# A scheduler's clock count, its refinements, and two buffers, in a state-space scan followed by window attention

## The chip, the cores and the metric

The kernel runs on one core of a Trainium2 chip, in float32. The metric is the time of one execution on the device in microseconds; lower is better. Each kernel is run several times, and the median counts. One execution per kernel is also recorded by the hardware profiler. In the profile PE is TensorE's products, PEld its weight loads, DVE is VectorE, ACT ScalarE, POOL GpSimd, and SP the engine that issues the transfers.

## The reference, cut to what matters

Input x is 8 images of 192 channels, 64x64. Two layers follow each other.

```python
# layer 0
x  = conv1x1(x, W_in)                     # 192 -> 384 channels
x  = depthwise3x3(x) + b_dw
p  = conv1x1(x, W_xd)                     # 16 values per point
ws, Ls, Us, Ds = (conv1x1(p, w) for w in (W_w, W_l, W_u, W_d))
xs = stack(x, x.T, flip(x), flip(x.T))    # 4 directions x 384 channels
Gl, Gm, Gr = split(ws)
s  = abs(Gl) + abs(Gm) + abs(Gr) + 1e-7   # each gate is divided by s
for t in range(8):                        # steps within chunks of 8 columns
    h = Ls*xs + (Gl*h_up + Gm*h + Gr*h_dn) / s
    out[t] = h*Us + xs*Ds
y  = sum over directions of w_m[d] * out[d]
y  = layernorm over channels(y)
y  = grn(y)                               # needs the sum of y*y over the image
x  = conv1x1(y, W_out)                    # 384 -> 192

# layer 1
s0 = layernorm(tokens of x)
for each window of 8x8 tokens, for each of 6 heads:
    a = l2norm(q) @ l2norm(k).T * temperature
    a = where(a >= 16th largest of its row, a, -100)
    o = softmax(a + rpb) @ v
x2 = s0 + proj(o)
out = x2 + fc2(gelu(fc1(layernorm(x2))))  # 192 -> 768 -> 192
```

## The kernel before

**Three streams.** For each image there is a *front* (input projection, depthwise convolution as products on TensorE over strips read back from DRAM), a *scan*, and eight *window rows* of attention and feed-forward, each 8 image rows of 512 tokens. While image b is scanned, the front of image b+1 and the window rows of image b-1 are written beside it. The window rows of an image can begin only when its scan has ended, since the normalisation needs a sum over the whole image.

**The scan.** A tile is one direction, 128 channels and 512 points at one step t: 12 tiles a step, 8 steps an image, 768 tiles in all. For t above 0 a tile goes so. TensorE makes four products, three into PSUM banks named g and one into the bank nb (`gates`, L681); nb comes from a pool of two banks of its own (`n_ps`), all others of a pool of six. DVE multiplies by the input (L730) and by the state (L745, L747), ACT takes absolute values (L738, L760), POOL adds two of them (L769), DVE the third into nb (L777), so nb holds the normaliser. ACT makes the first reciprocal (L780, L782), POOL adds the products and multiplies (L784, L788, L799), DVE refines (L795, L803) and writes the new state (L810). After every second tile TensorE makes four output products for the pair (`both`, in `outputs`), and DVE (L836, L841) and POOL (L848 to L858) add them to the sum over directions.

**The window rows.** In order: scaling and W_out (L1040, L1055), normalisation, transposes (L1020), q and k (L1105), v (L1144), normalising q and k (L1179), their transposes (L1192, copied out by L1200), scores (L1220), top 16 on DVE (L1247 to L1264), softmax, transposes (L1321), product with v (L1341), projection (L1375), norm, transposes (L1443, L1445), widening (L1462, L1466) into `hd`, gelu (L1482), narrowing (L1496) and output.

**What sets the order.** None of this is issued in the order in which it is written. Each step is noted with its engine, its cost and the buffers that it reads and writes (`plan`, class `Plan`); a buffer is a `Held`, made by its first user and given back when its last user in the plan has run. `Plan.order` then lays out all steps with a list scheduler: on each engine it takes, of the steps that can start soonest, the one with the lowest rank. After each run a step's rank is set to the start of what needs it first, less its own length, and the plan is run again, `RUNS` times; the shortest is kept. All five engines' instructions are issued in that order. The hardware's semaphores are put in from what the instructions really touch, so a wait that only the plan has shapes the order and nothing else.

**The clock in the plan.** A PE step has a cost of a lead in ns, a number of cycles, and a share. `run` counts `cycles * share` in windows of `TICK` ns; in a window whose predecessor counted `ENTRY` or more, PE runs at 2.4 cycles per ns, else at 1.2. The costs are lambdas near L460: `mm`, `tiled`, `split`, `turned`, `mg`.

**The two buffers.** `outputs` got the second tile's `nb` and named it as read by the step `both`, though the function `both` does not touch it. The transposed q and k of a row lay in two buffers of tag `four`, 96 partitions of 2 x 512 values each; the hidden layer `hd` is one buffer of 128 x 6 x 512.

Of the kernel before, what the change touches and what calls it, by code (L numbers as in the profile page):

```python
# [54 lines left out]
class Held:  # L55
# [11 lines left out]
    def __call__(self):  # L67
        return self.tile
# [9 lines left out]
class Plan:  # L78
# [5 lines left out]


    HOP = 35.0
    TICK, ENTRY = 10240 / 3, 3060.0
    RUNS = 12
    SLACK = 40.0

    def __init__(self):
# [1 line left out]
        self.parts = {}  # L93
        self.rank, self.lane = 0.0, 0

    def __call__(self, engine, cost, fn, r=(), w=()):
        s = Step(engine, fn, cost, self.rank, self.lane, len(self.steps))
        self.steps.append(s)
        deps = set()
        for item in r:  # L100
            for k in self._overlaps(item, self.writers):
                deps.update(self.writers[k])
        for item in w:
            for k in self._overlaps(item, self.writers):
                deps.update(self.writers[k])
            for k in self._overlaps(item, self.readers):
                deps.update(self.readers[k])
        for item in list(r) + list(w):
            h = item[0] if isinstance(item, tuple) else item
            if isinstance(h, Held) and s not in h.users:  # L110
                if not h.users:
                    s.makes.append(h)
                else:
                    deps.add(h.users[0])
                h.users.append(s)
                s.held.append(h)
                h.left += 1
        for item in w:
            for k in self._overlaps(item, self.readers):
                if k == item or not isinstance(item, tuple):  # L120
                    self.readers[k] = []
            if not isinstance(item, tuple):
                for k in self._overlaps(item, self.writers):
                    self.writers[k] = []
            self.writers[item] = [s]
        for item in r:
            self.readers.setdefault(item, []).append(s)
        self._index(list(r) + list(w))
        deps.discard(s)
        s.before = len(deps)  # L130
        for d in deps:
            d.after.append(s)
        return s
# [12 lines left out]
    def order(self):  # L146

        before = [s.before for s in self.steps]
        tiles = {h: h.left for s in self.steps for h in s.held}
        best = None
        for _ in range(self.RUNS):
            for s, k in zip(self.steps, before):
                s.before, s.ready = k, 0.0
            for h, k in tiles.items():
                h.left, h.end, h.next = k, 0.0, None  # L160
            run = self.run()
            if best is None or self.length < best[0]:
                best = self.length, run, [s.start for s in run]
            for s in run:
                needs = [d.start for d in s.after] + [h.next.start for h in s.held if h.next]
                s.rank = min(needs, default=s.end) - (s.end - s.start)
        self.length, run, starts = best
        for s, t in zip(run, starts):
            s.start = t
        return run  # L170
# [118 lines left out]
def tile_ss2d_then_window_attention(ctx: ExitStack, tc: tile.TileContext, a: dict, out: bass.AP):  # L289
# [170 lines left out]
    vec = lambda n: (n / 0.96 + 69, 88)  # L460
    act = lambda n, more=50.0: (n / 1.2 + more, 110)
    gp = lambda n: (n * 2.3 + 52, 42)
    mm = lambda slots, n, share=1.0: (65.0, slots * n * 4.16, share)
    tiled = lambda cycles, share=1.0: (150.0, cycles, share)
    split = (275.0, 6475.0, 1.0)
    turned = lambda n, share=1.0: (60.0, 262.0 * n, share)

    mg = lambda share=1.0: (120.0, 2270.0, share)
    dma = lambda n=1, kb=0: (max(350.0 * n, 5.4 * kb), 2600.0)
    tiny = (150.0, 60.0)  # L470
    log_c = {}
# [144 lines left out]
    def scan(b, xs, xsT, z, made):  # L616
# [68 lines left out]
        def tile_of(t, d, ct, xp, x0, y3, last):  # L685
# [85 lines left out]
            if last:  # L771
                last()

            def rest():
                if t > 0:
                    rr = Held(spool, [P, 512], "rr", bufs=2)
                    plan("DVE", vec(512), lambda: nc.vector.tensor_add(nb(), nb(), ab()[:, 0, :]), r=[ab], w=[nb])  # L777

                    plan(
                        "ACT", (581.0, 110.0), lambda: nc.scalar.activation(rr(), nb(), AF.Ln, bias=eps7), r=[nb], w=[rr]  # L780
                    )
                    plan("ACT", act(512, 95.0), lambda: nc.scalar.activation(rr(), rr(), AF.Exp, scale=-1.0), w=[rr])  # L782
                    one = lambda: pr()[:, 0, :]
                    plan("POOL", gp(512), lambda: nc.gpsimd.tensor_add(one(), one(), pr()[:, 1, :]), r=[(pr, 1)], w=[(pr, 0)])  # L784
                    plan(
                        "POOL",
                        gp(512),
                        lambda: nc.gpsimd.tensor_add(one(), one(), pr()[:, 2, :]),  # L788
                        r=[(pr, 2)],
                        w=[(pr, 0)],  # L790
                    )
                    plan(
                        "DVE",
                        vec(512),
                        lambda: nc.vector.scalar_tensor_tensor(nb(), nb(), 1e-7, rr(), ALU.add, ALU.mult),  # L795
                        r=[rr],
                        w=[nb],
                    )
                    plan("POOL", gp(512), lambda: nc.gpsimd.tensor_mul(one(), one(), rr()), r=[rr], w=[(pr, 0)])  # L799
                    plan(  # L800
                        "DVE",
                        vec(512),
                        lambda: nc.vector.scalar_tensor_tensor(nb(), nb(), 2.0, one(), ALU.subtract, ALU.mult),  # L803
                        r=[(pr, 0)],
                        w=[nb],
                    )
                    plan(
                        "DVE",
                        vec(512),
                        lambda: nc.vector.tensor_sub(state(d, ct), like(lx(), d), like(nb(), d)),  # L810
                        r=[lx, nb],
                        w=[h_key],
                    )
                waiting.append((d, ct, xd, xv, h_key))
                if len(waiting) == 2:
                    outputs(waiting, nb if t > 0 else None)

            def outputs(pair, nb):

                banks = [[bank("g") for _ in range(2)] for _ in range(2)]  # L820

                at = PAIRS.index(tuple(p[:2] for p in pair)) * P

                def both():
                    for k in range(2):
                        for m in range(2):
                            project(banks[k][m](), w_g2, 64 * k + RG * m, RG, at, xp())

                plan("PE", mg(), both, r=[xp, nb] if nb else [xp], w=banks[0] + banks[1])
                for (d, ct, xd, xv, h_key), (pd, pu) in zip(pair, banks):  # L830
                    onto_sum(d, ct, xd, xv, h_key, pd, pu)
                pair.clear()
# [31 lines left out]
        def norm(t, y3):  # L864
# [22 lines left out]
            m4 = Held(spool, [P, P], "m4", tag="xq", bufs=1)  # L887
            plan("PE", tiled(1553.0), lambda: means(pm, y3), r=[y3], w=[pm])
            plan("ACT", act(P), lambda: nc.scalar.copy(m4(), pm()[:, 0:P]), r=[pm], w=[m4])
            plan("PE", tiled(2203.0), lambda: spread(pm, m4), r=[m4], w=[pm])  # L890
            plan(
                "DVE",
                vec(1536),
# [26 lines left out]
                r=[pv],  # L920
                w=[sq],
            )
            plan("PE", tiled(2203.0), lambda: spread(pv, rr), r=[sq], w=[pv])
            plan(
                "DVE",
                vec(1536),
# [85 lines left out]
    def window_row(b, g, z, sc, bb):  # L1012
# [170 lines left out]
        plan("DVE", (2373.0, 90.0), unit, r=[nn], w=[qk])  # L1183
        yield
        plan.lane = 8
        qkT = [Held(lpool, [HALF, 2, GT], "four", bufs=2) for _ in range(2)]
        for k in range(4):
            pt = bank()

            def turn(k=k, pt=pt):  # L1190
# [2 lines left out]
                        pt()[0:HALF, tt * P : (tt + 1) * P], qk()[:, tt, k * HALF : (k + 1) * HALF], ident  # L1193
                    )

            plan("PE", turned(4), turn, r=[qk], w=[pt, (qkT[k // 2], "room")])
            plan(
                "ACT",
                act(512),
                lambda k=k, pt=pt: nc.scalar.copy(qkT[k // 2]()[:, k % 2, :], pt()[0:HALF, :]),  # L1200
                r=[pt],
                w=[(qkT[k // 2], k % 2)],
            )
            yield

# [8 lines left out]
        def scores():  # L1214
            for w in range(WS):
                tok = slice(w * 64, w * 64 + 64)
                for r in range(3):
                    rows = slice(32 * r, 32 * r + 32)
                    for j in range(2):
                        nc.tensor.matmul(  # L1220
                            pas[r]()[64 * j : 64 * j + 64, tok],
                            lhsT=qkT[0]()[rows, j, tok],
                            rhs=qkT[1]()[rows, j, tok],
                            start=True,
                            stop=True,
                        )

        plan("PE", tiled(2550.0, 0.6), scores, r=qkT, w=pas + [(at, "room")])
        for r in range(3):
            rng = slice(r * WS, (r + 1) * WS)  # L1230
            plan(
# [114 lines left out]
                                stop=True,  # L1346
                            )

        plan("PE", tiled(2350.0, 0.5), attend, r=[at, v], w=po + [("oT", "room")])
        for w in range(2):  # L1350
            plan(
                "ACT",
# [288 lines left out]
```

## Time and profile before

| | |
|---|---|
| median of 3 runs | 7846.2 us (7838.49 to 7853.48) |
| the profiled execution | 7831.69 us, its span 7829.6 us |
| mean granted TensorE clock | 0.849 |
| busy PE, PEld | 6807.6, 3516.3 us |
| busy DVE, ACT, POOL | 6279.8, 4911.0, 6212.0 us |
| instructions | 144584 |
| read and written in HBM | 453.43 and 232.67 MB |

Busy times are the union of an engine's instructions. The ends of products are modelled, so a busy PE is not PE at its peak; the granted clock says in tenths of full speed at what rate it ran. In the list of waits each line has the waiting engine, tile and line, then what ended the wait, then us in total, number of waits and the longest. Line numbers are those of the kernel before.

### The profile page before, as it was taken

Reading aid. Unit: us, or ns where it says so; the run is one execution under the profiler, and the core shown is the slowest. Engines: PE = TensorE matmul, PEld = TensorE weight load, DVE = VectorE, ACT = ScalarE, POOL = GpSimd, SP = SyncE. Lnnn points to the kernel's source line nnn. Section 1 sums busy time; section 2 is a strip of 40 time slices with the busy share of each in tenths; the row PEclk is TensorE's granted clock in tenths of the full one; section 3 lists DMA queues with packets and bytes.
Section 4 is the critical chain, followed back from the end, with each engine's and each line's share of the span. In section 5 each row is a group of like instructions: output and inputs, shape, how many; then the busy total and the mean of one; then the engine's idle time right before and its main releaser. Section 6 shows DMA issues by size and latency. Waiting matters only on the chain.

```text
span 7829.6 us, 144584 instructions
## 1 busy us (share of the span) xinstructions
PE 6807.6 (87%) x51224; PEld 3516.3 (45%) x51224; DVE 6279.8 (80%) x15421; ACT 4911.0 (63%) x9657; POOL 6212.0 (79%) x6302
## 2 busy tenths in 40 slices
PE   5788888888999889889998889988888898788888
PEld 2333344444444444444444444444444444344554
DVE  1377778899788978889889888888899989999443
ACT  1355446775666656766677656767566656666665
POOL 0388878899788978888889878888799989899332
PEclk8788779987898878888898779988878878788998
DMA  7666445312543135322553124431211121111110
GB/s 183 181 170 167 125 123 146 100 50 65 151 115 78 47 112 137 87 69 59 140 141 85 44 85 129 115 80 51 58 48 49 50 61 51 46 47 46 25 25 14
DMA packets 1037929, 695.53 MB, mean 89 GB/s; under 512 B 704116, under 2 KB 860215, under 8 KB 1037207
## 3 DMA queue, kind: packets, MB, share of 16 engines
q1 hardware_dynamic: 1035830, 684.99, 33.0%
q8 instruction: 407, 6.67, 0.4%
q14 instruction: 316, 2.58, 0.1%
q10 hardware_dynamic: 1376, 1.30, 0.1%
HBM read 453.43 MB, written 232.67 MB: 88 GB/s over the span
## 4 chain that ended last, share of the span: by engine, by line
DVE 21%; PE 19%; POOL 15%; ACT 8%; issue 4%; DMA 0%; POOLq 0%; SPq 0%; ACTq 0%; DVEq 0%
PE g L681 6%; PE lp L1496 4%; POOL pr L799 3%; POOL ab L769 2%; POOL pr L784 2%; DVE rest L1249 2%; POOL dx L850 2%; PE lp L1105 2%; POOL pr L788 2%; DVE pr L745 2%; DVE nb L803 1%; DVE pr L747 1%; PE lp L1462 1%; POOL y L858 1%; DVE top L1247 1%
## 5 line engine op out<-in xcount | busy, mean ns | idle before, releaser
L681 PE MATMUL g<-xe,w_g 32*128 32x512 f32 x3648 | 1273.0, 768 | 271.1 <-DVE dx L836 106.9
L681 PE MATMUL g<-xo,w_g 32*128 32x512 f32 x3648 | 1156.1, 728 | 218.5 <-DVE dx L836 123.8
L784 POOL TENSOR_TENSOR pr<-pr 128x512 f32<-128x512 f32 x672 | 878.0, 1307 | 192.7 <-DVE pr L745 137.1
L769 POOL TENSOR_TENSOR ab<-ab 128x512 f32<-128x512 f32 x672 | 873.3, 1300 | 162.6 <-ACT ab L738 157.8
L738 ACT ACTIVATE ab<-g 128x512 f32<-128x512 f32 x1344 | 782.2, 596 | 333.3 <-PE nb L681 145.7
L799 POOL TENSOR_TENSOR pr<-pr,rr 128x512 f32<-128x512 f32 x672 | 869.2, 1294 | 125.7 <-ACT rr L782 106.9
L788 POOL TENSOR_TENSOR pr<-pr 128x512 f32<-128x512 f32 x672 | 865.4, 1289 | 17.2
L850 POOL TENSOR_TENSOR dx<-dx,hu 128x512 f32<-128x512 f32 x576 | 738.2, 1290 | 121.8 <-DVE hu L841 108.2
L780 ACT ACTIVATE rr<-nb,eps 128x512 f32<-128x512 f32 x672 | 461.3, 686 | 566.5 <-DVE nb L777 564.4
L681 PEld LDWEIGHTS g<-xe,w_g 32*128 32x128 f32 x3648 | 447.3, 216 | 811.2 <-DVE dx L836 227.8
L568 PE MATMUL lp<-strip,w_cv 128*32 128x256 f32 x9216 | 682.0, 440 | 142.5 <-DMA strip<-pad 123.5
L681 PEld LDWEIGHTS g<-xo,w_g 32*128 32x128 f32 x3648 | 390.9, 206 | 731.5 <-DVE dx L836 250.2
L1496 PE MATMUL lp<-hd,w_f 128*64 128x256 f32 (+1 forms) x2304 | 585.1, 492 | 33.7 <-ACT hd L1482 23.6
L795 DVE SCALAR_TENSOR_TENSOR nb<-nb,rr 128x512 f32<-128x512 f32 x672 | 464.5, 691 | 186.8 <-ACT rr L782 185.9
L858 POOL TENSOR_TENSOR y<-y,dx 128x512 f32<-128x512 f32 x384 | 593.4, 1554 | 2.2
L803 DVE SCALAR_TENSOR_TENSOR nb<-nb,pr 128x512 f32<-128x512 f32 x672 | 464.4, 691 | 152.0 <-POOL pr L799 149.7
L777 DVE TENSOR_TENSOR nb<-nb,ab 128x512 f32<-128x512 f32 x672 | 464.5, 691 | 110.3 <-POOL ab L769 94.2
L568 PEld LDWEIGHTS lp<-strip,w_cv 128*32 128x32 f32 x9216 | 304.5, 123 | 543.0 <-issue 274.3
L848 POOL TENSOR_TENSOR y<-hu,dx 128x512 f32<-128x512 f32 x192 | 252.6, 1320 | 340.6 <-DVE hu L841 337.9
L841 DVE TENSOR_TENSOR hu<-g,hid 128x512 f32<-128x512 f32 x768 | 517.8, 678 | 4.9 <-PE g L681 4.4
L681 PE MATMUL nb<-xe,w_g 32*128 32x512 f32 x672 | 511.9, 852 | 11.1 <-DVE hid L810 8.8
L760 ACT ACTIVATE nb<-nb 128x512 f32<-128x512 f32 x672 | 398.7, 593 | 183.6 <-DVE pr L745 107.7
(203 smaller groups left out, 16680.0 us busy)
## 6 DMA issues: line engine op xcount, KB each, us to landing
strip<-pad SPq DMA_DIRECT2D x1152, 132.0 KB
xd<-xsT SPq DMA_DIRECT2D x384, 256.0 KB
pad<-xin SPq DMA_DIRECT2D x192, 264.0 KB
xs<-st SPq DMA_DIRECT2D x192, 256.0 KB
xsT<-sn SPq DMA_DIRECT2D x192, 256.0 KB
xd<-xs SPq DMA_DIRECT2D x192, 256.0 KB
x<-xs SPq DMA_DIRECT2D x64, 768.0 KB
z<-y SPq DMA_DIRECT2D x64, 768.0 KB
```

The costliest lines, as they stand in the source:

```text
L568: nc.tensor.matmul(pc()[q * RG : (q + 1) * RG, k * 256 : (k + 1) * 256].rearrange("p (h w) -> p h w", h=4), lhsT=w_cv[:, ct, q, dx, :], rh ...
L681: nc.tensor.matmul(dst, lhsT=w[rows, col : col + P], rhs=xp[rows, :], start=True, stop=True)
L738: lambda r=r: nc.scalar.activation(ab()[:, r, :], g[r](), AF.Abs),
L769: plan("POOL", gp(512), lambda: nc.gpsimd.tensor_add(ab()[:, 0, :], ab()[:, 0, :], ab()[:, 1, :]), w=[ab])
L784: plan("POOL", gp(512), lambda: nc.gpsimd.tensor_add(one(), one(), pr()[:, 1, :]), r=[(pr, 1)], w=[(pr, 0)])
L788: lambda: nc.gpsimd.tensor_add(one(), one(), pr()[:, 2, :]),
L799: plan("POOL", gp(512), lambda: nc.gpsimd.tensor_mul(one(), one(), rr()), r=[rr], w=[(pr, 0)])
L803: lambda: nc.vector.scalar_tensor_tensor(nb(), nb(), 2.0, one(), ALU.subtract, ALU.mult),
L841: lambda: nc.vector.tensor_mul(like(hu(), d), like(pu(), d), state(d, ct)),
L850: plan("POOL", gp(512), lambda: nc.gpsimd.tensor_add(dx(), dx(), hu()), r=[hu], w=[dx])
L858: nc.gpsimd.tensor_add(y, y, dx().rearrange("p (c i) -> p i c", c=CH))
L1496: nc.tensor.matmul(dst[:, at : at + rhs.shape[-1]], lhsT=lhsT, rhs=rhs, **flags)
```

## The change

The planner's shares: full products from 1.0 to 0.96, 0.95 or 0.9, two kinds of `tiled` to 0.93, the product with v from 0.5 to 0.65. `ENTRY` goes from 3060 to 3200. `RUNS` goes from 12 to 30, and from the second run on a rank is the mean of the old and the new. `plan` takes steps in `behind`, after which a step must come without a buffer between them: `both` is now put behind the step that made the last value of nb (L803), and no longer holds nb. The four transposed blocks of q and k become one buffer of 96 x 4 x 512 under the tag `hd`, the same single buffer that the hidden layer uses.

```diff
-    TICK, ENTRY = 10240 / 3, 3060.0
-    RUNS = 12
+    TICK, ENTRY = 10240 / 3, 3200.0
+    RUNS = 30
...
-    def __call__(self, engine, cost, fn, r=(), w=()):
+    def __call__(self, engine, cost, fn, r=(), w=(), behind=()):
...
-        deps = set()
+        deps = set(behind)
...
-        for _ in range(self.RUNS):
+        for n in range(self.RUNS):
...
-                s.rank = min(needs, default=s.end) - (s.end - s.start)
+                rank = min(needs, default=s.end) - (s.end - s.start)
+                s.rank = (s.rank + rank) / 2 if n else rank
...
-    mm = lambda slots, n, share=1.0: (65.0, slots * n * 4.16, share)
+    mm = lambda slots, n, share=0.96: (65.0, slots * n * 4.16, share)
...
-    split = (275.0, 6475.0, 1.0)
+    split = (275.0, 6475.0, 0.95)
...
-    mg = lambda share=1.0: (120.0, 2270.0, share)
+    mg = lambda share=0.9: (120.0, 2270.0, share)
...
+            made_w = []
...
-                    plan(
-                        "DVE",
-                        vec(512),
-                        lambda: nc.vector.scalar_tensor_tensor(nb(), nb(), 2.0, one(), ALU.subtract, ALU.mult),
-                        r=[(pr, 0)],
-                        w=[nb],
+                    made_w.append(
+                        plan(
+                            "DVE",
+                            vec(512),
+                            lambda: nc.vector.scalar_tensor_tensor(nb(), nb(), 2.0, one(), ALU.subtract, ALU.mult),
+                            r=[(pr, 0)],
+                            w=[nb],
+                        )
                     )
...
-                    outputs(waiting, nb if t > 0 else None)
+                    outputs(waiting, made_w)
...
-                plan("PE", mg(), both, r=[xp, nb] if nb else [xp], w=banks[0] + banks[1])
+                plan("PE", mg(), both, r=[xp], w=banks[0] + banks[1], behind=made_w)
...
-            plan("PE", tiled(2203.0), lambda: spread(pm, m4), r=[m4], w=[pm])
+            plan("PE", tiled(2203.0, 0.93), lambda: spread(pm, m4), r=[m4], w=[pm])
...
-            plan("PE", tiled(2203.0), lambda: spread(pv, rr), r=[sq], w=[pv])
+            plan("PE", tiled(2203.0, 0.93), lambda: spread(pv, rr), r=[sq], w=[pv])
...
-        qkT = [Held(lpool, [HALF, 2, GT], "four", bufs=2) for _ in range(2)]
+        qkT = Held(lpool, [HALF, 4, GT], "four", bufs=1, tag="hd")
...
-            plan("PE", turned(4), turn, r=[qk], w=[pt, (qkT[k // 2], "room")])
+            plan("PE", turned(4), turn, r=[qk], w=[pt, (qkT, "room")])
...
-        plan("PE", tiled(2550.0, 0.6), scores, r=qkT, w=pas + [(at, "room")])
+        plan("PE", tiled(2550.0, 0.6), scores, r=[qkT], w=pas + [(at, "room")])
...
-        plan("PE", tiled(2350.0, 0.5), attend, r=[at, v], w=po + [("oT", "room")])
+        plan("PE", tiled(2350.0, 0.65), attend, r=[at, v], w=po + [("oT", "room")])
```

## The prediction

> **What bounds the kernel now.** I read the page from the top, then the busy time by stretches, then the waits of VectorE and TensorE.
>
> ```profile
> span 7829.6 us, 144584 instructions
> ## 1 busy us (share of the span) xinstructions
> PE 6807.6 (87%) x51224; PEld 3516.3 (45%) x51224; DVE 6279.8 (80%) x15421; ACT 4911.0 (63%) x9657; POOL 6212.0 (79%) x6302
> ...
> PEclk8788779987898878888898779988878878788998
> ...
> DVE 21%; PE 19%; POOL 15%; ACT 8%; issue 4%; DMA 0%; POOLq 0%; SPq 0%; ACTq 0%; DVEq 0%
> ```
>
> No engine is full. PE leads at 87%, DVE and POOL follow at 80 and 79%, and the chain that ended last runs over all three, none with more than 21%. DMA holds none of it. The TensorE clock is below full in every slice. So time is lost where engines take turns, which is what an order of instructions decides.
>
> ```profile
> core 0: us, PE busy (x) PEld busy (x) DVE busy (x) ACT busy (x) POOL busy (x), PEclk, DMA share, GB/s
> 330.00:1200.00 870.00, 735.61 (x4910) 319.90 (x4910) 667.98 (x1065) 460.32 (x824) 726.38 (x592) 0.77 0.56 148
> ...
> 3000.00:3900.00 900.00, 821.28 (x6255) 424.06 (x6255) 778.09 (x1906) 601.13 (x1177) 774.14 (x775) 0.87 0.35 93
> ...
> 5700.00:6600.00 900.00, 791.10 (x5352) 417.71 (x5349) 822.68 (x2067) 598.83 (x1204) 816.53 (x834) 0.83 0.18 51
> ...
> 7253.00:7830.00 577.00, 483.40 (x4461) 306.79 (x4460) 262.88 (x1282) 364.87 (x779) 169.64 (x363) 0.91 0.10 22
> ```
>
> Four stages with different limits: the first image's scan without attention beside it (clock 0.77); the steady part (PE 91%, DVE and POOL 86%); from 5700 us, when the front has no image left, DVE and POOL at 91% and PE at 88%; and after the last scan update at 7253 us a tail of 577 us in which PE is busy 84% and the others much less.
>
> ```profile
> ACT rr L780 <- DVE nb L777: 564.4, 356, 8.1
> ...
> PE g L681 <- DVE dx L836: 230.7, 142, 6.7
> ...
> DVE nb L795 <- ACT rr L782: 185.9, 159, 4.4
> ...
> DVE nb L803 <- POOL pr L799: 149.7, 162, 4.2
> ...
> ACT four L1200 <- PE lp L1192: 55.6, 51, 3.5
> ...
> PE nb L681 <- DVE hid L810: 19.4, 14, 3.1
> ```
>
> The numbers after the colon are us in total, times, and the longest. ScalarE's 564 us are its own slack (63% busy). What costs are DVE's waits inside a tile (L795, L803), and PE waiting until DVE has read a bank (L836). PE's wait for the normaliser's bank, the one that the change speaks of, is 19.4 us in all.
>
> **The change part by part.** I compared the two instruction orders engine by engine. The same instructions are there on every engine (26,894 TensorE products before splitting, 13,887 on DVE, 9,221 on ACT, 6,305 on POOL, 2,966 on SP): nothing is added or taken away, no DMA either. Everything is order, so each part is costed by what it does to the order.
>
> *The normaliser's bank.* The product step of a pair never touches the bank in its code; naming it only kept the planner from reusing the bank early. The chip has no such wait to lose. At most PE's 19.4 us for that bank (and 51.5 us of weight loads) could change; at least nothing. The order says nothing: at 376 of 384 pairs exactly one further tile's gates stand ahead of the pair's products, before and after, and the gates follow the products at once 312 times before and 311 after. Value 0.
>
> *One buffer for the transposed q, k and the hidden layer.* It adds a wait: the copies into it (L1200) and behind them the scores, the top-k on DVE and the mask may not start while the hidden layer of the row before is in use. In the old order 9 of 63 rows overlapped so. In the new one 62 rows have their scores ahead of the first widening product and one follows the last narrowing product, so the wait lies satisfied in PE's own order. A row held back by the life of the hidden layer (4.4 tiles on average; 768 tiles in 6,908 us are 9.0 us each, so 40 us) costs only if the last rows are later. Eleven rows' wide layers are left when the scan's last product is issued, in both orders. Value 0; bounds 0 and one row more in the tail, 577/11 = 52 us.
>
> *The clock's counting.* It takes no cycle from PE; it only tells the planner which windows run at full rate. From the trace I summed, over the 3.413 us windows between the recorded clock changes, the cycles of each step by the planner's own table. Threshold 3060 with the old shares foresees the next window's rate in 94.5% and calls 71.5% full; 69.6% were. Threshold 3200 with the new shares: 93.9%, and 65.1% full. So the new planner takes PE for somewhat slower than it is, an error that gives PE's steps room and costs no more than that room. Here the page "TensorE: Matmul & The Clock Gate" of the Trainium skill speaks against the change (Part 1, on the HAM clock gate): the window runs freely and isn't reset when a kernel starts, and the warm-up costs under 1% of a typical kernel's span. By the first, no plan can aim at windows counted from its own time zero, and I follow it: value 0 by intent. By the second no clock effect could pass 78 us. Here the trace differs: mean clock 0.849, so some 30% of the time is at half rate. If half of the time is bound by PE (58 of 110 six-tile stretches below), 0.01 of clock is worth 0.01/0.849 of 6,908 x 58/110, or 43 us. I keep that for the range.
>
> *30 refinements, ranks averaged.* Here the order itself is the only evidence. I gave each instruction its mean duration from the trace's groups (PE's scaled to its 6,807.6 us busy) and measured three things in both orders.
>
> Balance: cut the scan into stretches of N tiles, take for each the engine with the most work, and add up. N=2: 7134 before, 7120 after; N=4: 6767 and 6769; N=6: 6534 and 6509; N=12: 6325 and 6309. The differences are -14, +2, -25, -16 us. Four tiles' inputs can be waiting beside a pair that waits for its outputs, so I lean to six: -20 us.
>
> Cover on DVE: between L777 and L795 of a tile the work of ACT (0.69 + 0.63 us and two handovers of 0.15, as the timeline has them, 1.62 us together) must be hidden by other DVE work. The shortfall summed over 672 tiles is 123 us in the old order (the trace shows 185.9) and 134 in the new. From L777 to L803 (POOL's 1.29 us more) it is 61 and 71. That is 10 us more; DVE is the fullest engine in a quarter of the stretches, and partly elsewhere, so I take +4 us. On POOL (L769 to L799) 23 and 25: nothing. For PE's banks, the time until a bank comes round again falls short by 429 and 424 us: nothing.
>
> Tail: of PE's work 455.7 us stood behind the last scan product and now 444.3, so 11.4 us go into the body. At 84% busy that shortens the tail by 13 us and lengthens the body, bound by PE about half of the time, by 6: -7 us. The head is the same: the same products stand ahead of the first scan product.
>
> Sum: -20 + 4 - 7 + 0 = -23 us. The profiled execution took 7831.7 us (span 7829.6 and 2.1 around it) and would become 7808.7. The median of the runs before is 14.5 us above that execution, so against it: 7846.2 - 23 = **7823 us**, 0.3% less.
>
> **The rivals.**
>
> *The clock comes out higher.* If the reordering closes gaps between products, more windows count as busy. For it: every slice of the page has half-rate windows, and the first scan runs at 0.77. Against it: the density of products is nearly the same (gaps of no other step between two scan steps: 473 before, 461 after). At 0.01 more clock it gives 7823 - 43 = 7780 us; at 0.02, 7737.
>
> *Slower: thinner cover in DVE's queue.* A plan is shorter because dependent steps stand closer. Between L777 and L803 of a tile there are 6.44 us of other DVE work before and 6.30 after, 0.14 us less in each of 672 tiles, 94 us in sum. The plan thinks that this is free; on the chip products and activations come at times shifted by a clock window, and a wait then opens at L795 or L803. With half of it paid, the term of +4 becomes +47, the sum +20, and the time 7866 us; with all of it 7913. It decides from the point where those two waits grow by more than the 27 us that balance and tail bring. For it: these two waits are already 336 us. Against it: ACT is idle 37% of the time, and most tiles have cover to spare.
>
> *The change doesn't do what it says.* The early bank and the shared buffer leave no mark in the order; then they count nothing and the time is the forecast's, from ranks alone. I hold this to be so.
>
> **How the numbers follow.** Forecast (small gain from ranks and tail) 0.52, own range 7795 to 7850; higher clock 0.26; thinner cover 0.22. A measurement of this kernel tells about 0.2%, 16 us, from no change. Faster by more than that (under 7830.5): 0.36 of the forecast's chance and all 0.26 of the clock's, 0.62. Slower by more (over 7861.9): 0.20 of the cover's and 0.02 of the forecast's, 0.22. Between: 0.16. The range goes down through the clock case to a little past its 0.01 (7765) and up past the half-paid cover (7880), short of a whole row more in the tail; about 0.1 lies beyond each end.
>
> **What would show it.** Right: busy times and counts of every group as before within a few us; the last scan update (L810) near 7240 us instead of 7253.5; the tail about 565 us; waits at L795 and L803 together within 20 us of 336; clock 0.845 to 0.855. Wrong for the forecast: clock of 0.86 or more with a PE busy time well under 6,800 us (the clock case), or those two waits above 380 us with DVE's busy time unchanged (the cover case). L1200 or L1473 waiting for the shared buffer, or a tail of over 600 us, would say that the buffer costs after all. PE's wait for L810 staying near 19 us would confirm that freeing the bank early does nothing.

## The result and the profile after

The changed kernel takes 7777.7 us (median of 4 runs, 7769.28 to 7784.22) against 7842.3 for the kernel before in the same runs: ratio 0.9918, 95% interval 0.9899 to 0.9937. So it is 0.8% faster, about 64 us. The forecast was 0.3% faster and a range from 7765 to 7880: the side and the range hold, the size is well under half. The profiled execution took 7776.0 us.

The page of the changed kernel, span, busy times, clock and chain:

```profile
span 7774.2 us, 144512 instructions
## 1 busy us (share of the span) xinstructions
PE 6784.8 (87%) x51224; PEld 3499.8 (45%) x51224; DVE 6280.8 (81%) x15421; ACT 4902.0 (63%) x9657; POOL 6208.0 (80%) x6302
...
PEclk8888778888898889888898889988788878888998
...
DVE 29%; PE 29%; POOL 20%; ACT 9%; issue 6%; DMA 1%; SPq 0%; POOLq 0%; DVEq 0%; ACTq 0%
```

The chain of before adds up to 67% of the span and this one to 94%, so their shares can't be compared. The counts of instructions on the five compute rows are the same, and the busy times of DVE, ACT and POOL agree within 9 us. Nothing became cheaper; the same work lies closer together. PE has 23 us less busy time at a mean clock of 0.853 (0.849 before).

Where the time went is seen by cutting both executions at the first and the last state update of the scan. These are the stretches between them, before and then after (columns: stretch, length, busy us of PE, PEld, DVE, ACT, POOL, clock, DMA share, GB/s):

```profile
345.50:7253.50 6908.00, 6102.43 (x44990) 3108.46 (x44990) 5963.56 (x14032) 4471.86 (x8772) 6007.50 (x5908) 0.85 0.34 90
```

```profile
337.80:7217.40 6879.60, 6097.55 (x45042) 3104.68 (x45045) 5965.19 (x14038) 4466.64 (x8782) 6003.27 (x5910) 0.85 0.34 90
```

The first update starts 7.7 us earlier, the stretch is 28.4 us shorter with DVE and POOL as busy as before within 5 us (DVE's idle time falls from 944 to 914 us), and what follows the start of the last update shrinks from 576 to 557 us. By stage after the change:

```profile
core 0: us, PE busy (x) PEld busy (x) DVE busy (x) ACT busy (x) POOL busy (x), PEclk, DMA share, GB/s
330.00:1200.00 870.00, 715.96 (x4958) 308.32 (x4947) 676.48 (x1101) 464.45 (x833) 734.58 (x604) 0.79 0.57 150
...
3000.00:3900.00 900.00, 823.49 (x6404) 422.44 (x6406) 786.74 (x1926) 604.40 (x1205) 781.67 (x789) 0.87 0.37 98
...
5700.00:6600.00 900.00, 788.83 (x5594) 426.05 (x5589) 818.12 (x2072) 596.06 (x1218) 812.67 (x834) 0.84 0.19 52
...
7218.00:7774.00 556.00, 473.50 (x4406) 297.83 (x4402) 261.41 (x1275) 360.72 (x767) 168.78 (x361) 0.92 0.10 22
```

In the first scan DVE and POOL get some 8 us more work done in the same 870 us, at a clock of 0.79 instead of 0.77, and in the steady part 9 and 8 us more in the same 900 us; in the stage without a front they get no more. The tail has 10 us less of PE's work. The waits after (lines moved by 1 to 5):

```profile
ACT rr L783 <- DVE nb L780: 577.2, 367, 7.5
...
PE g L682 <- DVE dx L841: 201.1, 116, 7.7
...
DVE nb L798 <- ACT rr L785: 187.1, 161, 3.9
...
DVE nb L807 <- POOL pr L802: 162.6, 174, 4.1
...
ACT four L1205 <- PE lp L1197: 67.5, 59, 3.7
...
PE nb L682 <- DVE hid L815: 16.6, 12, 3.3
```

The two waits inside a tile come to 350 us (336 before), PE's wait for a bank that DVE has to read to 201 (231), and the wait for the normaliser's bank to 16.6 (19.4). One of DVE's waits in the window rows is shorter too, that for the squares of q and k, before and then after:

```profile
DVE nn L1128 <- ACT sq L1121: 187.8, 71, 19.6
```

```profile
DVE nn L1133 <- ACT sq L1126: 164.7, 88, 14.1
```

So two waits fell by 23 and 30 us, others rose, and none accounts for the 64 us.

### The profile page after: what moved, and what is told of

Same layout as the page of the kernel before. It is cut to its first block, busy times and chain, and to the rows that moved or that the text cites. A ratio compares the mean times of both kernels' runs of the same rounds, so it can differ in the third digit from the quotient of the medians.

```text
span 7774.2 us, 144512 instructions
## 1 busy us (share of the span) xinstructions
PE 6784.8 (87%) x51224; PEld 3499.8 (45%) x51224; DVE 6280.8 (81%) x15421; ACT 4902.0 (63%) x9657; POOL 6208.0 (80%) x6302
## 4 chain that ended last, share of the span: by engine, by line
DVE 29%; PE 29%; POOL 20%; ACT 9%; issue 6%; DMA 1%; SPq 0%; POOLq 0%; DVEq 0%; ACTq 0%
PE g L682 9%; PE lp L1501 5%; POOL pr L802 4%; POOL ab L770 3%; POOL pr L787 3%; POOL pr L791 3%; POOL dx L855 3%; DVE pr L746 3%; DVE rest L1254 2%; PE lp L1110 2%; DVE nb L807 2%; PE lp L569 2%; DVE pr L748 2%; DVE hid L815 2%; DVE nb L780 2%
## 5 line engine op out<-in xcount | busy, mean ns | idle before, releaser
L682 PE MATMUL g<-xe,w_g 32*128 32x512 f32 x3648 | 1234.9, 756 | 267.7 <-DVE dx L841 98.0
L682 PEld LDWEIGHTS g<-xe,w_g 32*128 32x128 f32 x3648 | 424.8, 212 | 799.2 <-DVE dx L841 198.1
L569 PE MATMUL lp<-strip,w_cv 128*32 128x256 f32 x9216 | 666.0, 430 | 124.6 <-DMA strip<-pad 114.6
```

The lines of the kernel that those rows point to most:

```text
L569: nc.tensor.matmul(pc()[q * RG : (q + 1) * RG, k * 256 : (k + 1) * 256].rearrange("p (h w) -> p h w", h=4), lhsT=w_cv[:, ct, q, dx, :], rh ...
L682: nc.tensor.matmul(dst, lhsT=w[rows, col : col + P], rhs=xp[rows, :], start=True, stop=True)
```

## The experiments

Ratios are to the kernel before, measured on the same chip beside each kernel. The first four take one part of the change alone.

**The clock's count alone.**

```diff
-    TICK, ENTRY = 10240 / 3, 3060.0
+    TICK, ENTRY = 10240 / 3, 3200.0
-    mm = lambda slots, n, share=1.0: (65.0, slots * n * 4.16, share)
+    mm = lambda slots, n, share=0.96: (65.0, slots * n * 4.16, share)
...
```

> The kernel before with the new threshold (3200) and shares alone; 12 refinements, ranks not averaged, both buffers as before. Ranks theory (the prediction's: the gain is from the refinements, the clock's count is worth nothing): within 15 us of before, 7827 to 7857. Clock theory (the stricter count lays a better order): most of the 65 us, 7770 to 7795. Shuffle theory (every new order is a draw, parts do not add): anything from 7800 to 7880. Followed through the plan's own arithmetic, this order is 51 us longer than before's under the old constants and 76 us shorter under the new ones, so the sign tells which constants describe the chip.

Measured: 7847.8 us, ratio 1.0001 (0.9992 to 1.0009). The count alone brings nothing; the clock theory falls in its plain form. The sign that was to tell which constants describe the chip didn't come, neither +51 nor -76.

**The refinements alone.**

```diff
-    RUNS = 12
+    RUNS = 30
...
+                s.rank = (s.rank + rank) / 2 if n else rank
```

> The kernel before with 30 refinements and averaged ranks alone. Ranks theory: all of the gain, 7775 to 7800. Clock theory: within 15 us of before. Shuffle theory: 7800 to 7880. The plan's arithmetic says 27 us shorter than before under the old constants, 62 us shorter under the new.

Measured: 7817.7 us, ratio 0.9966 (0.9954 to 0.9978): 27 us, less than half of the gain. Both the theory that gives all of it to the ranks and the plain clock theory fall; the range of the shuffle theory holds.

**The normaliser's bank alone.**

```diff
-                plan("PE", mg(), both, r=[xp, nb] if nb else [xp], w=banks[0] + banks[1])
+                plan("PE", mg(), both, r=[xp], w=banks[0] + banks[1], behind=made_w)
```

> The kernel before with only the normaliser's bank given back by the output products (they stand behind the last write to it instead). Ranks and clock theory: no wait of the chip is touched, so within 15 us of before. Shuffle theory: it moves all the same, since the order is laid anew, by more than 15 us either way. The plan's arithmetic: 3 us longer under the old constants, 38 us shorter under the new.

Measured: 7834.5 us, ratio 0.9989 (0.9979 to 0.9999). About 9 us, at the edge of what can be told from nothing. The shuffle theory asked for more than 15 us either way, and misses.

**The shared buffer alone.**

```diff
-        qkT = [Held(lpool, [HALF, 2, GT], "four", bufs=2) for _ in range(2)]
+        qkT = Held(lpool, [HALF, 4, GT], "four", bufs=1, tag="hd")
```

> The kernel before with only the transposed q and k moved into the hidden layer's buffer. Ranks and clock theory: value 0, within 15 us of before; if the shared buffer costs, slower by up to 52 us. Shuffle theory: moves by more than 15 us either way. The plan's arithmetic: 14 us shorter under the old constants, 7 us shorter under the new.

Measured: 7834.9 us, ratio 0.9988 (0.9981 to 0.9996). The buffer costs nothing, and brings about 9 us; here too the shuffle theory misses. The four parts together make some 44 us of the 64.

The next four undo one part of the full change; each edit is one of the above taken back.

**Without the clock's count.**

```diff
-    TICK, ENTRY = 10240 / 3, 3200.0
+    TICK, ENTRY = 10240 / 3, 3060.0
...
```

> The changed kernel with the old threshold (3060) and shares put back. The single parts measured -0.34% (refinements), -0.11% (bank), -0.12% (buffer) and +0.01% (clock). If parts add: the same as the three others, -0.57% or 7799, whether the clock's part is there or not; the changed kernel's further 20 us are then a draw. If the clock's count pays only with refinements that can follow it: back to 7820 or more. The plan's arithmetic says 89 us shorter than before under the old constants and 75 under the new, the only order so far that both call shorter by that much: 7755 to 7775 if it is to be trusted.

Measured: 7776.0 us, ratio 0.9916 (0.9904 to 0.9928), the same as the full change. As given, the new threshold and shares are worth nothing with the other parts either. But the three other parts, which alone make 45 us, make 66 together: parts don't add.

**Without the bank.**

```diff
-                plan("PE", mg(), both, r=[xp], w=banks[0] + banks[1], behind=made_w)
+                plan("PE", mg(), both, r=[xp, nb] if nb else [xp], w=banks[0] + banks[1])
```

> The changed kernel with the output products holding the normaliser's bank in the plan again. If parts add: it loses 0.11%, about 9 us, 7786. If the early bank is what lets the refinements work: 7815 or more. The plan's arithmetic: 24 us shorter than before under the old constants, 198 under the new; half way is 111, 7733.

Measured: 7798.3 us, ratio 0.9943 (0.9931 to 0.9955): some 20 us lost, with intervals that just touch those of the full change, where adding the parts said 9 and the plan's half way said a gain.

**Without the shared buffer.**

```diff
-        qkT = Held(lpool, [HALF, 4, GT], "four", bufs=1, tag="hd")
+        qkT = [Held(lpool, [HALF, 2, GT], "four", bufs=2) for _ in range(2)]
```

> The changed kernel with the transposed q and k in their own two buffers again. If parts add: loses 0.12%, about 9 us, 7787. If the constraint is what steers the window rows into a better order: 7815 or more. The plan's arithmetic: 85 us longer than before under the old constants, 99 shorter under the new; half way is 7 shorter, 7836.

Measured: 7876.7 us, ratio 1.0041 (1.0028 to 1.0054). Slower than the kernel before, with every other part in. The buffer that brought 9 us alone seems worth 97 here.

**Without the refinements.**

```diff
-    RUNS = 30
+    RUNS = 12
...
-                s.rank = (s.rank + rank) / 2 if n else rank
+                s.rank = rank
```

> The changed kernel with 12 refinements and ranks not averaged. If parts add: loses 0.34%, 27 us, 7805. If the refinements carry all: 7842 within 15. If they only pick a draw: anywhere, 7780 to 7850. The plan's arithmetic: 34 us longer than before under the old constants, 134 shorter under the new; half way is 50 shorter, 7792.

Measured: 7809.6 us, ratio 0.9959 (0.9946 to 0.9971). Some 32 us lost: adding the parts asked for 27, and a draw allowed it too. That the refinements carry all falls.

So adding the parts comes near for two of these four, the refinements and the bank, and fails for the other two by 23 and 90 us: the buffer is worth 9 us or 97. Two explanations stay. Either sharing the buffer steers the refined order, or each edit lays a new order and the orders differ in quality. For the second I followed the order that each kernel issues through the plan's own arithmetic, under three counts of the clock: the old constants, the new ones, and the new shares with the threshold at 2920, where the count foresees the clock recorded in the trace of before in 95.1% of windows. This last was settled before the four runs that follow.

**Refinements and bank, no shared buffer, old count.**

```diff
-    RUNS = 12
+    RUNS = 30
...
+                plan("PE", mg(), both, r=[xp], w=banks[0] + banks[1], behind=made_w)
```

> The kernel before with the refinements and the early bank; shares and threshold old, q and k in their own two buffers. Buffer theory (sharing the buffer steers the rows, and without it the refined order is bad, as in the run without the buffer): 7840 or more. Parts add: -0.34 and -0.11%, 7805. Plan theory (a kept order is as good as its length in the plan's arithmetic under a threshold that fits the trace, whichever part it came from): with the new shares and threshold 2920, at which the count foresees the recorded clock best, this order is 75 us shorter than before's, so 7765 to 7790.

Measured: 7804.7 us, ratio 0.995 (0.9938 to 0.9963). Faster than before without the buffer: the buffer theory falls, as far as a kernel with the old count can tell. The parts' sum hits it, and the plan theory asked for more than came.

**The threshold that fits the trace**, the rest as in the changed kernel.

```diff
-    TICK, ENTRY = 10240 / 3, 3200.0
+    TICK, ENTRY = 10240 / 3, 2920.0
```

> The changed kernel with its threshold at 2920 instead of 3200, at which the new shares foresee the clock in before's trace best (95.1% of windows). Clock-is-worth-nothing theory: as the changed kernel, within 15 us of 7778. Plan theory: its order is 133 us shorter than before's by that count (71 by the old constants, 119 by the new), against 31 for the changed kernel's; the first eight orders gave the chip some 0.8 of such a difference: 7730 to 7750. Shuffle theory: 7770 to 7880.

Measured: 7735.8 us, ratio 0.9865 (0.9852 to 0.9878), 42 us better than the changed kernel and inside the range of the plan theory.

**Old shares, threshold 3140, 60 refinements**, as an edit to the kernel without the clock's count.

```diff
-    TICK, ENTRY = 10240 / 3, 3060.0
-    RUNS = 30
+    TICK, ENTRY = 10240 / 3, 3140.0
+    RUNS = 60
```

> Refinements, bank and buffer as in the changed kernel, with the old shares, threshold 3140 and 60 refinements: a try at a better version. Plan theory: shorter than before's order by 89, 113, 106 and 143 us under four sets of constants (old, new, new shares with 2920, old shares with 3140), the only order so far that all of them call short by over 85: 7735 to 7765. Clock-is-worth-nothing theory and more refinements with no further use: 7776 within 15.

Measured: 7738.0 us, ratio 0.9866 (0.9847 to 0.9885). Inside the plan theory's range again; what the 60 refinements and what the threshold bring isn't separated. These two orders are better than the kernel before and the changed one by more than the intervals.

**Without the shared buffer, on another path**, as an edit to the kernel without the shared buffer.

```diff
-    HOP = 35.0
+    HOP = 36.0
```

> The changed kernel with q and k in their own two buffers, as in the run that was slower by 0.41%, and the plan's allowance for a handover between engines at 36 ns instead of 35, which means nothing for the chip and only makes the refinements take another path. Buffer theory: slow again, 7860 to 7890. Plan theory: this order is 20 us shorter than before's (the slow one was 44 longer) with the new shares and threshold 2920: 7815 to 7840. Shuffle theory: anywhere from 7780 to 7880.

Measured: 7801.7 us, ratio 0.9943 (0.993 to 0.9957). One nanosecond in the plan, which the chip never sees, is worth 0.98% or 77 us. The buffer theory falls with the new count too; the plan theory's range is missed by 13 us, on the fast side, and the shuffle theory's holds. The slow order and this one between their first and last state updates:

```profile
342.60:7300.50 6957.90, 6134.97 (x45026) 3125.30 (x45022) 5978.89 (x14038) 4464.05 (x8786) 6006.21 (x5910) 0.84 0.34 89
```

```profile
339.50:7253.70 6914.20, 6125.11 (x45179) 3125.93 (x45178) 5976.91 (x14042) 4468.17 (x8791) 6022.90 (x5916) 0.85 0.34 90
```

And the order with the threshold at 2920:

```profile
341.10:7195.40 6854.30, 6097.77 (x45150) 3115.16 (x45152) 5977.99 (x14043) 4465.80 (x8790) 6009.23 (x5916) 0.85 0.34 90
```

DVE's busy time is within 16 us in all five stretches shown and ACT's within 8, while the length goes from 6958 to 6854 us. For DVE and ACT what differs is idle time alone: DVE's goes from 979 to 876 us. PE's busy time falls as well, from 6135 to 6098 us, at 0.843 and 0.853 of the clock over these two executions. The waits of DVE in the slow order and in the best, over the whole execution, show where; the slow one first:

```profile
DVE nb L798 <- ACT rr L785: 193.6, 163, 3.7
DVE nb L807 <- POOL pr L802: 185.0, 181, 5.0
DVE nn L1133 <- ACT sq L1126: 182.7, 68, 18.6
DVE nb L780 <- POOL ab L770: 115.2, 117, 5.0
```

```profile
DVE nb L798 <- ACT rr L785: 170.1, 153, 3.2
DVE nb L807 <- POOL pr L802: 165.0, 180, 6.1
DVE nn L1133 <- ACT sq L1126: 144.9, 70, 7.7
DVE nb L780 <- POOL ab L770: 95.4, 110, 3.9
```

Each wait is 11 to 21% shorter and none is gone; the four make 101 us of the 135 by which DVE is idle less over the whole execution. Three belong to a tile of the scan, one to the window rows.

All orders together, as difference to the order of before, in us. The first three columns are the plan's arithmetic; the last is the ratio less one, times 7842:

| order | old constants | new constants | new shares, 2920 | chip |
|---|---|---|---|---|
| clock alone | +51 | -75 | +20 | +1 |
| refinements alone | -27 | -61 | -31 | -27 |
| bank alone | +3 | -38 | -27 | -9 |
| buffer alone | -14 | -7 | -3 | -9 |
| the change | +7 | -116 | -31 | -64 |
| without clock | -89 | -75 | -58 | -66 |
| without bank | -24 | -198 | -62 | -45 |
| without buffer | +85 | -99 | +44 | +32 |
| without refinements | +34 | -133 | -24 | -32 |
| refinements and bank | -92 | -65 | -75 | -39 |
| threshold 2920 | -72 | -119 | -133 | -106 |
| old shares, 3140, 60 | -89 | -113 | -106 | -105 |
| without buffer again | +34 | -109 | -21 | -45 |

The correlation with the chip is 0.91 for the third column, 0.74 for the first and 0.37 for the second. The constants of the change are the worst of the three at telling good orders from bad: by them the order without the bank is the best of all, and on the chip it is in the middle. With a line through the third column the chip is off by 16 us in the root mean square; for the change's own order the plan says 31 us and the chip gives 64, which stays unexplained. Of the four ranges that the third column gave ahead of the runs two held; of the other two, one asked for more than came and one for less.

Is it the clock? The orders differ in it, by the median over each one's executions: 0.847 before, 0.853 after, 0.857 with old shares and 3140. Faster orders mostly have the higher clock (correlation of time and clock -0.72). But the refinements with the bank ran at 0.843 and gained 39 us, and without the buffer it was 0.848 and 32 us were lost. The executions of one kernel vary in clock too, with the order held: over 139 executions of the fourteen kernels the time falls by 26 us for 0.01 of clock (95% interval 20 to 33). By that, the 0.006 that the change has more would go with 16 of its 64 us. So the clock is a part of it and not the most; what raises it in one order and not in another isn't shown.

## Why the prediction was right or wrong

**What bounds the kernel: right.** Three engines below full taking turns, and only the order to gain from. All thirteen orders bear it out: over the profiled executions of the fourteen kernels the busy times of DVE, ACT and POOL lie within 29, 20 and 17 us, and the spans within 140. The shares of the chain, none over 21%, were weaker evidence than they seemed, since that chain covers only 67% of the span.

**The clock's count at 0: right for the change as made** (1.0001 alone, 0.9916 without against 0.9918 with). The reason given, the freely running window of the Trainium skill's page "TensorE: Matmul & The Clock Gate" (Part 1), was too strong. The traces agree that the window isn't tied to the kernel's start: from there to the first clock change it is 27.9 us before and 30.1 after, which leaves 0.60 and 2.84 us over whole windows of 3.413 us. Yet the plan's arithmetic, which counts its windows from its own start, goes with the measured times at a correlation of 0.91 with the threshold at 2920, and the order laid with that threshold is 42 us better than the change's.

I had the comparison of thresholds in the prediction (94.5% against 93.9%), called the error harmless, and did not ask what a right threshold would bring. Whether the 42 us are due to the better count or to a luckier path through the refinements isn't separated: a path alone moved 77 us. The table speaks for the first, though the three counts lie close together: they foresee 93.9, 94.5 and 95.1% of the windows, and go with correlations of 0.37, 0.74 and 0.91. The bound of 78 us was a misreading: that page's rule of under 1% speaks of the warm-up, and here half-rate windows lie all over the execution and make up 30.4% of before's trace and 29.6% of after's.

**The bank at 0: right on the chip's waits, not quite as a part.** PE's wait for it was 19.4 us and is 16.6. Alone the edit gives about 9 us; undone it costs 20. Both are within what a new path through the refinements gives.

**The buffer at 0: right that it costs nothing**, and that the scores stand ahead of the widening: after the change the two copies into the shared buffer (L1205, L1478) wait for PE's products, 67.5 and 149.2 us, and no wait for the buffer shows. Its apparent 97 us are mostly a matter of paths: two orders without it lie 77 us apart.

**Refinements and order: the term that was mis-sized.** The sum was -23 us, and the refinements alone measured -27; that the two agree is luck, since the sum was worked out from the order of the whole change. That order gave -55 in the profiled executions. Against the sum: the head was called the same and came 7.7 us earlier; the body was put at -20 + 4 + 6 = -10 and came to -28; the tail at -13 and came to -19. The largest miss is the body, and in it the balance of stretches, put at -20. It counts how evenly work is shared and cannot see whether the shared work is ready, and its four readings, from +2 to -25, left the choice to me. That the balance fell short, and not the clock that was put at nothing, is argued and not shown. Nor is the split a fixed mark of the gain. The kernel without the clock's count is as fast, and its stretch between the updates is this:

```profile
351.90:7194.90 6843.00, 6094.61 (x44985) 3100.28 (x44980) 5968.89 (x14033) 4460.32 (x8774) 6000.00 (x5906) 0.85 0.34 90
```

It starts 6.4 us later than before's and is 65.0 us shorter, and its tail is 1.4 us shorter.

The cover on DVE was right in its sum, +10 us of shortfall and +14 in the two waits, but not in its place: the shortfall was to grow by 11 us already at L795, and the wait there grew by 1 and that at L803 by 13.

**The rivals.** The higher clock came in part: 0.004 more in the profiled executions and 0.006 by the medians, not 0.01. By the prediction's price 0.006 is 26 us, by the spread of executions 16. The thinner cover stayed under its point, 14 us against 27. That the early bank and the shared buffer leave no mark held for the structure I had counted, but not for the times.

## What to carry to other kernels

When a scheduler lays the order, an edit to its inputs can't be judged by undoing it: a nanosecond in a constant moved this kernel by 1%, so lay several orders on both sides before giving a part the credit. A planner's estimate is worth calibrating against a recorded trace (here by the share of clock windows that its count foresees), since one estimate went with the measured times at 0.91 where the one chosen did at 0.37. With engines at 80 to 87% and no dominant wait, look for gains in the search over orders and not in a single wait.

## What the runs showed of the hardware

Being busy in the profile isn't enough to win the full clock. The recorded clock is full or half and changes after whole windows of 3.413 us. In before's trace, of 452 half-rate windows in which PE was busy for 95% or more, only 58% were followed by a full-rate one. Counting the cycles of the products by the planner's table with the old shares orders these windows better: of all half-rate windows, under a tenth of those with 2600 to 2800 cycles were followed by full rate, under half of those with 3000 to 3200, and 97% or more above 3800. Orders with the same products can so have different clocks: by the medians 0.848 and 0.854 in the two without the shared buffer, though one order alone ranges from 0.843 to 0.850 over its five executions.
